# Messages turned by a matmul with the scaled W_o1 in place of a transpose, and an end stretch that joins gelu on POOL

## The chip, the cores and the metric

The kernel runs on one core of a Trainium2 chip. It is measured by the device time of one execution, in microseconds; the median of the runs counts. A core has a matrix engine (PE, with its weight loads shown apart as PEld), a vector engine (DVE), a scalar engine (ACT), a general engine (POOL) and an engine that issues transfers (SP). They run side by side, each in the order of its own instructions, and wait for one another by semaphores. PE writes to PSUM; the other data on the chip is in SBUF.

## The reference

One layer of a graph network, with 12500 nodes of 128 features and 400000 edges sorted by destination (`dst`), in float32:

```python
h = maximum(layernorm(x), 0)
Wij = smu(edge_attr @ W_f1.T + b_f1) @ W_f2.T + b_f2      # edge_attr: (400000, 20)
Wij = Wij * edge_weight[:, None]
x_ij = (h @ W_in2f.T)[dst] * Wij
agg = segment_sum(x_ij, src, 12500)
out = x + smu(agg @ W_o1.T + b_o1) @ W_o2.T + b_o2
```

with `smu(x) = ((1 + a) x + (1 - a) x erf(m (1 - a) x)) / 2`, a = 0.01, m = 2.5. In the kernel this is a gelu plus a straight part: with z = ZS x, smu(x) = GC (gelu(z) + LIN x), where ZS, GC and LIN are constants made of a and m. GC is folded into the weights that follow.

The call takes `x` as (idx_j = dst, idx_i = src): rows of h are gathered by the sorted `dst`, and the sum goes over `src`, which is in no order.

## The kernel before

**Tiles.** The 400000 edges are 3125 tiles of 128. Four tiles are a *group* (782 of them), two groups a *super* (391). The nodes are 98 *bins* of 128. Since `src` has no order, the messages are sorted into bins through DRAM: each message row (128 features and its place in the bin) is scattered to a slot of its bin, and later each bin's rows are read back and summed by a matmul with a selection matrix. This goes by *epochs*: nine of them, of 59, 59, 59, 59, 48, 37, 27, 27 and 16 supers (so 118, 118, 118, 118, 96, 74, 54, 54 and 32 groups), each with a buffer of its own. While epoch k's messages are made and scattered, epoch k-1's are read back and summed. What epoch 8 scattered is read back in the *end stretch*, together with the output.

**A group in the main loop.** The loop over g works on several groups at once:

- `hide(g+2)`: PE, first filter product into `pu` (L551); `bend`: ACT, gelu into `ge` (L559); `smooth`: DVE, straight part added into `sm` (L567)
- `weigh(g+1)`: PE, second filter product into `pw` (L604); `gather(g+1)`: PE, rows of h by a one-hot matrix into `ph` (L585); `take`: ACT copies them to `hg` (L593); `mix(g+1)`: DVE, (pw + b2) * hg into `mt`, features on the partitions (L614)
- `turn(g)`: PE turns the four 128x128 blocks of `mt` into `pt`, edges on the partitions (L624)
- `send(g)`: ACT scales each edge's row by its edge weight into `ms`, which has six buffers (L634); POOL scatters the four tiles by four indirect DMAs (L637) to slots in `ix`
- `bins`, `count`, `read`, `number`: DVE and PE find the slots (L485, L499 to L502, L529, L538)
- `parts(k-1, ...)`: the sums of the epoch before. `fetch` loads `rw` (SP, L668), `choose` makes the selection matrices `se` (DVE, L679), `add` multiplies them (PE, L692) and adds four bins into `agg` (DVE, L705). They start four groups into an epoch (`WAIT`); `choose` for the first chunk stands two groups into it, and waits for the load, which waits for the last scatter of the epoch before.
- `step`: in epoch 0 alone, pieces of the preparation (layernorm, h, loads). `late_loads` is one of them.

Each engine has the order of these calls as written. `pt`, `pu`, `pw`, `ph` and `pc` have one PSUM bank each, `ge`, `sm`, `hg` and `mt` two buffers each.

**The end stretch.** A *unit* is four bins (24 of them) or one of the two last bins. In the loop over the bins of epoch 8, PE sums (L692), and for finished units, one behind the other:

- `first_half`: PE multiplies `agg` by `w_o1` into `pu` or `ph` (L250), ACT takes gelu into `ge` (L251)
- `between`: DVE adds LIN times the product to gelu, into `sm` (L255)
- `second_half`: PE multiplies by `w_o2` into `pw` or `pt` (L260)
- `store`: DVE adds the old rows of x (L264), SP writes out (L266, L268), and then `ask` loads the old rows for the unit four places on: issued by ACT's queue (L240) into `hg` or `mt`, output bias added by POOL (L246)

`between` and `store` are called after the second bin of a unit, `second_half` and `first_half` after the fourth, so a unit passes through three units' time.

**Opening.** Loads are issued from SP, ACT and POOL. `w_o1` is loaded in `late_loads`, from SP. DVE scales `w_f2` by GC there (L764). A path at the end of the program, taken only where a bound of the sorting is exceeded (not with this data), uses `half`, `bent`, `rest` and `stored` too.

Of the kernel before, what the change touches and what calls it, by code (L numbers as in the profile page):

```python
# [9 lines left out]
F32 = mybir.dt.float32  # L10
# [3 lines left out]
AF = mybir.ActivationFunctionType  # L14
ALU = mybir.AluOpType
# [4 lines left out]
P = 128  # L20
# [4 lines left out]
ZS = MU * (1.0 - ALPHA) * math.sqrt(2.0)  # L25
GC = (1.0 - ALPHA) / ZS
LIN = ALPHA / GC

SUP = 8
GRP = 4  # L30
# [9 lines left out]
def gnn_kernel(  # L40
# [19 lines left out]
    nc = tc.nc  # L60
# [9 lines left out]
    def bin_rows(t, b, n):  # L70
        return t[b * P:(b + n) * P, :].rearrange("(b p) f -> p b f", p=P)
# [34 lines left out]
    ident = const.tile([P, P], F32, name="ident")  # L106
# [42 lines left out]
    agg = const.tile([P, NB * P], F32, name="agg")  # L149
# [7 lines left out]
    bz = const.tile([P, 1], F32, name="bz")  # L157
    w_o1 = const.tile([P, P], F32, name="w_o1")
# [29 lines left out]
    def stats(pool, b):  # L188
        st = pool.tile([P, 6], F32, name="st")
        nc.vector.bn_stats(st, x_sb[:, b, :])  # L190
        nc.vector.bn_aggr(mv[:, b, :], st)
# [41 lines left out]
    def width(unit):  # L233
        b, n, rows = unit
        return (n - 1) * P + rows
# [12 lines left out]
    def half(unit, po, ge):  # L248
        w = width(unit)
        nc.tensor.matmul(po[:, :w], w_o1, agg[:, unit[0] * P:unit[0] * P + w], start=True, stop=True)  # L250
        nc.scalar.activation(ge[:, :w], po[:, :w], AF.Gelu, scale=ZS, bias=bz)  # L251

    def bent(unit, po, ge, sm):
        w = width(unit)
        nc.vector.scalar_tensor_tensor(sm[:, :w], po[:, :w], LIN, ge[:, :w], op0=ALU.mult, op1=ALU.add)  # L255

    def rest(unit, sm, py):
        b, n, rows = unit
        for j in range(n):
            nc.tensor.matmul(py[:rows, j, :], sm[:, j * P:j * P + rows], w_o2, start=True, stop=True)  # L260
# [10 lines left out]
    with tc.tile_pool(name="ld", bufs=4) as ld, \  # L271
# [110 lines left out]
        nc.gpsimd.dma_start(w_f1[0:R, :], w_f1_t)  # L382
        nc.gpsimd.dma_start(w_f1[R:R + 1, :], b_f1)
        nc.sync.dma_start(fbufs[0][0:R, :], f_t[:, 0:SUP * P])
        nc.scalar.dma_start(x_sb[:, 1:HEAD, :], bin_rows(x, 1, HEAD - 1))
        nc.gpsimd.dma_start(w_f2, w_f2_t)
        nc.gpsimd.dma_start(b2, b_f2.rearrange("o p -> p o"))
# [14 lines left out]
        def late_loads():  # L402

            nc.sync.dma_start(w_sb[:, CH:NT], w_col[:, CH:NT])
            nc.sync.dma_start(w_o1, w_o1_t)

        def later_loads():
            nc.sync.dma_start(w_o2, w_o2_t)
# [135 lines left out]
        def hide(g):  # L544

            if g >= NG:
                return
            n = groups[g][1] * P
            o = g % PER * GRP * P
            pu = ps1.tile([P, GRP * P], F32, name="pu")  # L550
            nc.tensor.matmul(pu[:, :n], w_f1, loaded[g // PER][0][:, o:o + n], start=True, stop=True)  # L551
            units_of[g] = pu
# [65 lines left out]
        def turn(g):  # L618

            n = groups[g][1]  # L620
            pt = ps1.tile([P, GRP, P], F32, name="pt")
            mt = mixed.pop(g)
            for j in range(n):
                nc.tensor.transpose(pt[:, j, :], mt[:, j * P:(j + 1) * P], ident)  # L624
            mixed[g] = pt

        def send(g):
# [134 lines left out]
        loaded[0] = (fbufs[0], None, h_first.rearrange("p b k d -> p (b k d)"))  # L762
        hide(0)
        nc.vector.tensor_scalar(w_f2, w_f2, GC, None, op0=ALU.mult)  # L764
        for b in range(1, HEAD):
            stats(edge, b)
        deviations(1, HEAD)
# [17 lines left out]
        for s in (1, 2):  # L785
            targets(s)
        turn(0)
        send(0)
        hide(1)
# [51 lines left out]
        for c in range(1, NC):  # L841
# [4 lines left out]
            for f in mine:  # L846
                steps.append(f)
                if c > 1:
                    steps.append(single.pop(0))
        steps += loads + [late_loads, later_loads, last_loads]  # L850
        for i in range(0, len(single), 2):
            steps.append(lambda two=single[i:i + 2]: [f() for f in two])
# [22 lines left out]
        for g in range(NG):  # L875
# [3 lines left out]
            i = g - g0  # L879
# [29 lines left out]
            if g:  # L909
                turn(g)  # L910
                send(g)
# [25 lines left out]
        row_of, ready, opened, smoothed, summed = [], [], [], [], []  # L937
# [11 lines left out]
        turns = [0, 0]  # L949

        def other(i, names):
            turns[i] += 1
            return names[turns[i] % 2]

        def first_half():
            unit = ready.pop(0)
            po = ps1.tile([P, GRP * P], F32, name=other(0, ("pu", "ph")))
            ge = edge.tile([P, GRP * P], F32, name="ge")
            half(unit, po, ge)
            opened.append((unit, po, ge))  # L960

        def between():
            unit, po, ge = opened.pop(0)
            sm = edge.tile([P, GRP * P], F32, name="sm")
            bent(unit, po, ge, sm)
            smoothed.append((unit, sm))

        def second_half():
            unit, sm = smoothed.pop(0)
            py = ps1.tile([P, GRP, P], F32, name=other(1, ("pw", "pt")))  # L970
            rest(unit, sm, py)
            summed.append((unit, py))

# [9 lines left out]
        for c in order_of[k]:  # L983
            for b in range(c * SPAN[k], min(NB, (c + 1) * SPAN[k])):
                for q in range(Q[k]):
                    add(k, b, q)
                if b % GRP == 1:
                    if opened:
                        between()
                    if summed:  # L990
                        store()
                if b % GRP == GRP - 1 or b == NB - 1:
                    ready += [u for u in units if u[0] // GRP == b // GRP]
                    if smoothed:
                        second_half()
                    if len(ready) > 1:
                        first_half()
        while ready or opened or smoothed or summed:
            if smoothed:
                second_half()  # L1000
            if ready:
                first_half()
            if opened:
                between()
            if summed:
                store()
# [16 lines left out]
    with tc.If(flag > 0):  # L1023
        with tc.tile_pool(name="gl", bufs=1) as gl, tc.tile_pool(name="gps", bufs=1, space=PSUM) as gps:
# [11 lines left out]
            with tc.For_i(0, NT, 1) as t:  # L1036
# [26 lines left out]
                                               op1=ALU.mult, accum_out=dup)  # L1063
                pu = gps.tile([P, P], F32, name="gpu")
                nc.tensor.matmul(pu, w_f1[:R + 1, :], fb, start=True, stop=True)
                ge = gl.tile([P, P], F32, name="gge")
                nc.scalar.activation(ge, pu, AF.Gelu, scale=ZS)
                sm = gl.tile([P, P], F32, name="gsm")
                nc.vector.scalar_tensor_tensor(sm, pu, LIN, ge, op0=ALU.mult, op1=ALU.add)
                pw = gps.tile([P, P], F32, name="gpw")  # L1070
# [17 lines left out]
            for b, n in chunks(NB, GRP):  # L1088
                pt = gps.tile([P, GRP * P], F32, name="gpt")
                w = min(N, (b + n) * P) - b * P  # L1090
# [6 lines left out]
        with tc.tile_pool(name="gfin", bufs=1) as fin, tc.tile_pool(name="gfps", bufs=1, space=PSUM) as fps:  # L1097
            for unit in units:
                xr, ys = fin.tile([P, GRP, P], F32, name="xr"), fin.tile([P, GRP, P], F32, name="ys")
                ge, sm = fin.tile([P, GRP * P], F32, name="fge"), fin.tile([P, GRP * P], F32, name="fsm")  # L1100
                po, py = fps.tile([P, GRP * P], F32, name="gpo"), fps.tile([P, GRP, P], F32, name="gpy")
                old_rows(unit, xr, nc.sync)
                with_bias(unit, xr, nc.vector)
                half(unit, po, ge)
                bent(unit, po, ge, sm)
                rest(unit, sm, py)
                stored(unit, py, xr, ys, nc.sync)
# [48 lines left out]
```

## Time and profile before

| | us |
|---|---|
| timed runs, median (three: 4150.53 to 4153.11) | 4151.15 |
| the profiled execution's own time | 4134.27 |
| its span, first to last instruction | 4132.4 |
| busy in it: PE / DVE / POOL / ACT | 3500.0 / 3498.8 / 3048.9 / 1854.6 |
| mean granted TensorE clock | 0.959 |

How to read it. A group line of the profile has the line of the kernel, engine and operation, the tiles it writes and reads, its shape, how many, then the busy time in us, the mean of one in ns, and the idle time of the engine just before them with what ended it. A stretch line has the stretch, its length, the busy time of each engine in it with the number of instructions, the granted clock, the DMA share and GB/s. A timeline line has the start, the duration, the engine and line, and in brackets the idle time before it. Matmuls are pipelined, so the step from one start to the next tells more than the duration of one. An f32 matmul appears as two records, a transpose as one.

POOL by epochs (all its work in the stretch between the starts of the epochs, as it scatters):

| stretch, us | what | PE busy | DVE busy | POOL busy |
|---|---|---|---|---|
| 655 to 1253 | epoch 1 | 505.60 | 497.46 | 454.07 |
| 2448 to 2935 | epoch 4 | 427.22 | 421.00 | 369.64 |
| 2935 to 3309 | epoch 5 | 336.16 | 330.94 | 283.75 |
| 3309 to 3584 | epoch 6 | 252.34 | 249.98 | 207.62 |
| 3584 to 3857 | epoch 7 | 235.34 | 239.84 | 207.11 |
| 3857 to 4024 | epoch 8 | 150.87 | 147.47 | 119.74 |
| 4024 to 4132.4 | end stretch | 92.79 | 74.43 | 32.07 |

### The profile page before, as it was taken

The page shows a single profiled execution, that of the slowest core. Times are in us where ns is not written, and L with a number is a line of the kernel's source. Part 1 is how long each engine was busy: PE and PEld are TensorE (multiplying, and loading weights), DVE is VectorE, ACT ScalarE, POOL GpSimd, SP SyncE. Part 2 cuts the span into 40 slices and gives each one's busy share as a digit, 9 for nine tenths or more (in the row PEclk, how much of TensorE's full clock was granted, in tenths as well). Part 3 has the DMA queues.
Part 4 walks back from the last instruction along what each step waited for, and adds up shares of the span by engine and source line. Part 5 has one row for each costly group of instructions (what it writes and reads, how often), then busy time and mean ns, then how long its engine had stood idle before and what let it go on. Part 6 is the DMA issues. An engine that isn't in the chain of part 4 may idle for free. (4 is left out here: it accounts for less than half of the span.)

```text
span 4132.4 us, 67973 instructions
## 1 busy us (share of the span) xinstructions
PE 3500.0 (85%) x18032; PEld 2218.3 (54%) x18032; DVE 3498.8 (85%) x8551; ACT 1854.6 (45%) x4810; POOL 3048.9 (74%) x3173
## 2 busy tenths in 40 slices
PE   6767886988887888869888879998799889898888
PEld 2334444555554555545555546665466556565567
DVE  6898886988887988869888869998799889898887
ACT  3446553544444444435444434444344444444431
POOL 4777777777777777777777777777777777777772
PEclk8999998999998999989999989999899999999999
DMA  4875665766656766647666647776588689787568
GB/s 144 234 198 174 189 186 176 211 193 193 196 156 200 211 197 190 199 140 214 214 189 194 201 149 209 215 212 199 173 233 230 176 244 248 211 234 219 170 184 240
DMA packets 564967, 820.60 MB, mean 199 GB/s; under 512 B 178779, under 2 KB 379234, under 8 KB 564444
## 3 DMA queue, kind: packets, MB, share of 16 engines
q1 hardware_dynamic: 450650, 602.06, 51.1%
q0 software_dynamic: 100320, 207.40, 15.2%
q10 hardware_dynamic: 13602, 6.73, 0.6%
q8 instruction: 143, 2.34, 0.3%
q14 instruction: 252, 2.06, 0.2%
HBM read 442.51 MB, written 373.37 MB: 197 GB/s over the span
## 5 line engine op out<-in xcount | busy, mean ns | idle before, releaser
L637 POOL DMA_INDIRECT buf<-ms,ix x3125 | 3008.6, 963 | 1006.6 <-issue 424.8
L634 ACT ACTIVATE ms<-pt,w_sb 128x128 f32<-128x128 f32 x3125 | 890.9, 368 | 1442.2 <-PE pt L624 848.6
L692 PEld LDWEIGHTS pg<-se,rw 128*128 128x128 f32 x8036 | 1060.6, 193 | 267.0 <-issue 225.1
L692 PE MATMUL pg<-se,rw 128*128 128x128 f32 x8036 | 1154.2, 281 | 8.5 <-DVE se L679 8.5
L485 DVE SCALAR_TENSOR_TENSOR so<-irow_ps,hi_f,so 128x98 f16<-128x98 f32 x3116 | 989.8, 318 | 82.6
L624 PE MATMUL pt<-ident,mt 128*128 128x128 f32 x3125 | 507.2, 286 | 524.7 <-DVE mt L614 522.0
L604 PE MATMUL pw<-sm,w_f 128*128 128x512 f32 x1564 | 902.9, 660 | 42.6 <-DVE sm L567 40.7
L551 PE MATMUL pu<-f,w_f 128*128 128x512 f32 x1564 | 824.5, 610 | 0.0
L559 ACT ACTIVATE ge<-pu 128x512 f32<-128x512 f32 x782 | 469.1, 600 | 555.4 <-PE pu L551 540.2
L679 DVE TENSOR_TENSOR se<-irow_ps,rw 128x1536 f32<-128x1536 f32 (+1 forms) x345 | 587.8, 1704 | 148.4 <-DMA rw<-buf 147.2
L614 DVE SCALAR_TENSOR_TENSOR mt<-pw,b,hg 128x512 f32<-128x512 f32 x782 | 583.3, 746 | 145.8 <-ACT hg L593 133.9
L624 PEld LDWEIGHTS pt<-ident,mt 128*128 128x128 f32 x3125 | 348.2, 143 | 624.5 <-DVE mt L614 618.2
L567 DVE SCALAR_TENSOR_TENSOR sm<-pu,ge 128x512 f32<-128x512 f32 x782 | 534.9, 684 | 151.6 <-ACT ge L559 147.1
L593 ACT ACTIVATE hg<-ph 128x512 f32<-128x512 f32 x782 | 469.1, 600 | 170.0 <-PE ph L585 99.6
L529 DVE TENSOR_REDUCE sl<-pc 128x4 f32<-128x392 f32 x782 | 434.7, 556 | 0.0
L604 PEld LDWEIGHTS pw<-sm,w_f 128*128 128x128 f32 x1564 | 240.3, 194 | 164.2 <-DVE sm L567 136.4
L585 PE MATMUL ph<-oh,hw 126*128 126x512 bf16 x776 | 306.4, 395 | 0.0
L551 PEld LDWEIGHTS pu<-f,w_f 128*128 128x128 f32 x1564 | 258.7, 199 | 59.5 <-issue 52.0
L499 PE MATMUL pc<-so,tri 128*128 128x392 f16 x782 | 260.6, 333 | 1.9 <-DVE so L485 1.1
L501 PE MATMUL pc<-so,rest_h 128*128 128x294 f16 x781 | 227.4, 291 | 0.0
L501 PEld LDWEIGHTS <-rest_h 128*128 128x128 f16 x781 | 77.1, 99 | 272.4 <-issue 272.3
L460 DVE TENSOR_SCALAR oh<-rbc,prow 128x1024 bf16<-128x1024 bf16 x388 | 192.8, 497 | 1.5 <-DMA rbc<-rel_dram 1.5
(151 smaller groups left out, 1357.5 us busy)
## 6 DMA issues: line engine op xcount, KB each, us to landing
rw<-buf SPq DMA_DIRECT2D x292, 774.0 KB
rbc<-rel_dram SPq DMA_DIRECT2D x389, 256.0 KB
buf<-zero SPq DMA_DIRECT2D x243, 387.0 KB
buf<-ms,ix POOLq DMA_INDIRECT x3125
buf<-zero SPq DMA_DIRECT2D x193, 258.0 KB
rw<-buf SPq DMA_DIRECT2D x49, 645.0 KB
f<-in_f_t SPq DMA_DIRECT2D x390, 80.0 KB
hw<-h_dram SPq DMA_DIRECT2D x776, 31.5 KB
```

The lines of the kernel that those rows point to most:

```text
L485: nc.vector.scalar_tensor_tensor(so[:, j], irow_ps[:, :NB], hi_f[:, t + j:t + j + 1], so[:, j - 1] if j else before, op0=ALU.is_equal, op1 ...
L551: nc.tensor.matmul(pu[:, :n], w_f1, loaded[g // PER][0][:, o:o + n], start=True, stop=True)
L559: nc.scalar.activation(ge[:, :n], units_of[g][:, :n], AF.Gelu, scale=ZS)
L567: nc.vector.scalar_tensor_tensor(sm[:, :n], units_of.pop(g)[:, :n], LIN, hidden[g][:, :n], op0=ALU.mult, op1=ALU.add)
L593: nc.scalar.activation(hg[:, :n], rows_of[g][:, :n], AF.Copy)
L604: nc.tensor.matmul(pw[:, :n], w_f2, hidden.pop(g)[:, :n], start=True, stop=True)
L614: nc.vector.scalar_tensor_tensor(mt[:, :n], pws.pop(g)[:, :n], b2, rows_of.pop(g)[:, :n], op0=ALU.add, op1=ALU.mult)
L624: nc.tensor.transpose(pt[:, j, :], mt[:, j * P:(j + 1) * P], ident)
L634: nc.scalar.activation(ms[:, j, 0:P], pt[:, j], AF.Copy, scale=w_sb[:, t + j:t + j + 1])
L637: i = nc.gpsimd.indirect_dma_start(out=bufs[k][:, :], out_offset=bass.IndirectOffsetOnAxis(ap=ix[:, j:j + 1], axis=0), in_=ms[:, j, :], in ...
L679: nc.vector.tensor_tensor(se[:, :m], irow_ps.unsqueeze(1).to_broadcast([P, m, P]), rows_in[c][:, :m, P:P + 1].to_broadcast([P, m, P]), op= ...
L692: nc.tensor.matmul(pgs[0][:, g, :], rows_in[c][:, o, 0:P], sel[c][:, o, :], start=(q == 0), stop=(q == Q[k] - 1))
```

## The change

W_o1 is applied to each message instead of to each node's sum: `turn` multiplies each block of `mt` by `w_o1` (scaled by LIN once at the opening) instead of turning it by the identity. What is scattered and summed is then LIN times the first output product, so `agg` holds what `pu` or `ph` held in the end stretch, times LIN. In the end stretch `first_half` has no product: ACT takes gelu from `agg` with the scale divided by LIN, and `between` adds `agg` to it on POOL instead of DVE. `second_half` goes around four PSUM banks instead of two. `w_o1` is loaded at the opening from ACT's queue, before the x rows of bins 1 to 3, and no longer from SP in `late_loads`. `half` and `bent`, now used only by the path not taken, have their scales changed to match.

```diff
@@ half, bent
-        nc.scalar.activation(ge[:, :w], po[:, :w], AF.Gelu, scale=ZS, bias=bz)
+        nc.scalar.activation(ge[:, :w], po[:, :w], AF.Gelu, scale=ZS / LIN, bias=bz)
...
-        nc.vector.scalar_tensor_tensor(sm[:, :w], po[:, :w], LIN, ge[:, :w], op0=ALU.mult, op1=ALU.add)
+        nc.vector.tensor_add(sm[:, :w], po[:, :w], ge[:, :w])
@@ opening
         nc.sync.dma_start(fbufs[0][0:R, :], f_t[:, 0:SUP * P])
+        nc.scalar.dma_start(w_o1, w_o1_t)
         nc.scalar.dma_start(x_sb[:, 1:HEAD, :], bin_rows(x, 1, HEAD - 1))
@@ late_loads
             nc.sync.dma_start(w_sb[:, CH:NT], w_col[:, CH:NT])
-            nc.sync.dma_start(w_o1, w_o1_t)
@@ turn
             for j in range(n):
-                nc.tensor.transpose(pt[:, j, :], mt[:, j * P:(j + 1) * P], ident)
+                nc.tensor.matmul(pt[:, j, :], mt[:, j * P:(j + 1) * P], w_o1, start=True, stop=True)
@@ opening
         nc.vector.tensor_scalar(w_f2, w_f2, GC, None, op0=ALU.mult)
+        nc.vector.tensor_scalar(w_o1, w_o1, LIN, None, op0=ALU.mult)
@@ end stretch
         def other(i, names):
             turns[i] += 1
-            return names[turns[i] % 2]
+            return names[turns[i] % len(names)]
+
+        def part_of(unit):
+            return agg[:, unit[0] * P:unit[0] * P + width(unit)]
 
         def first_half():
             unit = ready.pop(0)
-            po = ps1.tile([P, GRP * P], F32, name=other(0, ("pu", "ph")))
             ge = edge.tile([P, GRP * P], F32, name="ge")
-            half(unit, po, ge)
-            opened.append((unit, po, ge))
+            nc.scalar.activation(ge[:, :width(unit)], part_of(unit), AF.Gelu, scale=ZS / LIN, bias=bz)
+            opened.append((unit, ge))
 
         def between():
-            unit, po, ge = opened.pop(0)
+            unit, ge = opened.pop(0)
             sm = edge.tile([P, GRP * P], F32, name="sm")
-            bent(unit, po, ge, sm)
+            nc.gpsimd.tensor_add(sm[:, :width(unit)], part_of(unit), ge[:, :width(unit)])
             smoothed.append((unit, sm))
 
         def second_half():
             unit, sm = smoothed.pop(0)
-            py = ps1.tile([P, GRP, P], F32, name=other(1, ("pw", "pt")))
+            py = ps1.tile([P, GRP, P], F32, name=other(0, ("pu", "ph", "pw", "pt")))
             rest(unit, sm, py)
```

## The prediction

> **What bounds the kernel now.** I read the engines and groups of the page first, then one line at a time by stretches of the span, then the timelines of PE and of the end.
>
> ```profile
> PE 3500.0 (85%) x18032; PEld 2218.3 (54%) x18032; DVE 3498.8 (85%) x8551; ACT 1854.6 (45%) x4810; POOL 3048.9 (74%) x3173
> ...
> L637 POOL DMA_INDIRECT buf<-ms,ix x3125 | 3008.6, 963 | 1006.6 <-issue 424.8
> ...
> L692 PE MATMUL pg<-se,rw 128*128 128x128 f32 x8036 | 1154.2, 281 | 8.5 <-DVE se L679 8.5
> ...
> L624 PE MATMUL pt<-ident,mt 128*128 128x128 f32 x3125 | 507.2, 286 | 524.7 <-DVE mt L614 522.0
> ```
>
> POOL is at 74%, but its scatter does not stop. The same line by stretches:
>
> ```profile
> 670.00:770.00 100.00, 75.91 (x80) 1.00 0.69 202
> ...
> 2945.00:3065.00 120.00, 91.03 (x96) 0.99 0.81 231
> 3320.00:3440.00 120.00, 89.74 (x94) 0.98 0.90 247
> ...
> 3868.00:4012.00 144.00, 102.54 (x107) 0.99 0.68 202
> ```
>
> 120 us hold 96 scatters (91.0 us busy): about 1.26 us each (0.96 and a gap of 0.30, as POOL's timeline shows), 5.055 us for a group of four. 782 groups make 3953 of the 4132 us. So POOL sets the pace of the whole edge part, and PE, DVE and ACT run ahead of it until the six ms buffers are full (ACT's L634 waits 474 us for the scatter to release them). At 3320 and 3868 POOL falls short of its pace: there the producers are late.
>
> How late can they be? At each epoch's start PE loses its lead, as DVE's choose waits for rw until POOL has scattered the last group of the epoch before. From the starts of the L634 groups and of their scatters, the lead is some 20 to 24 us before the starts of epochs 2 to 6 (13, 8 and 14 before 1, 7 and 8), and 5 us after each (ACT L634 resumes at 2944.37 after a wait of 21.31 us, the scatter of that group is at 2950.05). From there the producers must beat 5.055 us a group. Their own pace after each restart, over 18 to 28 groups: epochs 1 to 3, 4.63; epoch 4, 4.81; 5, 4.78; 6, 5.07; 7, 4.79; 8, 5.39. In epoch 0 it is 5.00 (groups 20 to 110), against 5.14 for POOL there. The margin is 0.43 us in epochs 1 to 3, about 0.26 in 4, 5 and 7, none in 6 and 8.
>
> PE's timeline in such a run shows what a group is made of:
>
> ```profile
> 2957.26 1.12 PE L692 MATMUL pg<-se,rw 128*128 128x128 f32 x8
> 2958.22 0.60 PE L624 MATMUL pt<-ident,mt 128*128 128x128 f32 x4
> 2958.66 1.02 PE L604 MATMUL pw<-sm,w_f 128*128 128x512 f32 x2
> 2959.52 0.38 PE L585 MATMUL ph<-oh,hw 126*128 126x512 bf16 x1
> ```
>
> PE has no gap here. A transpose is one record (four of them x4), an f32 matmul two (L604 x2 for one product). Four transposes hold PE from 2958.22 to 2958.66: 0.44 us (0.50 in the group at 3029.61).
>
> **The change, part by part.** (1) *Four transposes become four f32 matmuls with the 128 columns of w_o1.* The nearest row has the same form, stationary slices of sm and 128 columns of w_o2 (L260), in the end stretch:
>
> ```profile
> 4100.94 1.13 PE L260 MATMUL pt<-w_o,sm 128*128 128x128 f32 x8
> ...
> 4101.91 1.02 PE L250 MATMUL pu<-agg,w_o 128*128 128x512 f32 x2
> ...
> 4102.77 1.95 PE L692 MATMUL pg<-se,rw 128*128 128x128 f32 x16
> ...
> 4104.59 1.13 PE L260 MATMUL pw<-w_o,sm 128*128 128x128 f32 x8
> ```
>
> Eight records, 4100.94 to 4101.91: 0.97 us. So +0.47 to +0.53, I take +0.50 us of PE in each of 782 groups. The first send of a group also comes 0.5 us later, which ACT (45% busy) covers.
>
> How much of the 0.50 reaches the pace? PE idles before L624, waiting for DVE's mt, by (idle of the group / number of groups in the window) 0.48 us a group in epoch 0 (58.6/122), 0.40 in 1 to 3, 0.38 in 4, 0.20 in 5, 0.24 in 6, 0.41 in 7, 0.09 in 8. It is concentrated in the groups in which DVE has a choose of 1.7 us (10 waits in 25 groups of epoch 5), and a later PE can swallow it there; in the other groups PE has none. At most all of that idle is swallowed, at least none. I take half, since after a swallowed group DVE's own slack is gone too. So the pace grows by 0.26, 0.30, 0.31, 0.40, 0.38, 0.30 and 0.45:
> - epoch 0: 5.26 against 5.14, 108 groups: +13
> - epochs 1 to 3: 4.93, under 5.055: 0. The lead no longer fills to 23 us, which costs nothing by itself
> - epoch 4: 5.12, 0.07 x 92: +6; epoch 5: 5.18, 0.13 x 70: +9
> - epoch 6: 5.45, 0.40 x 50: +20; epoch 7: 5.09, 0.04 x 50: +2
> - epoch 8, already on PE: 0.45 x 28: +13
> - the 5 us of lead can shrink to the 3.1 us seen in epoch 8 before POOL starves: -2 in each of 4, 5, 6: -6
>
> Main loop: +57. All idle swallowed: epochs 5, 6 and 8 alone, 2 + 14 + 11 - 4 = +23. None: 39 + 26 + 23 + 16 + 26 + 12 + 14 = +156.
>
> L624's rows have one record per block and L260's two, at about 0.11 to 0.12 us each, so the matmul costs twice the transpose here. [...]
>
> (2) *Scaling by LIN.* One DVE instruction of 0.22 us at the opening (row of w_f, L764), and the w_o1 load on ACT's queue, 0.45 us of issue ahead of the x rows. The x rows are used at 10.8 us, where DVE is behind anyway (its L721 waited until 9.0): 0 to +0.5 us, I take 0.3. One SP issue fewer in late_loads: nothing waits for it. Gelu's and the add's other scale cost nothing.
>
> (3) *The end stretch.* Removed are 24 wide products and two narrow ones: L250 holds PE 0.86 us of a unit's 3.65 us (4100.94 to 4104.59), with PE busy 100% from 4035 to 4115. If PE stayed the bound: -0.86 x 24 = -21. But DMA was busy 0.87, 0.97 and 0.84 in the three thirds of that stretch, which leaves some 10% of 80 us: -9 at best. And the add moves to POOL, a new wait. POOL's order is then add(k), bias(k+3), add(k+1), bias(k+4). A bias (L246) waits for its x rows, whose buffer (hg, mt, two each) is released by the store four units before. So add(k+1) stands behind a load that could be issued only after store(k-1), and store(k+1) needs add(k+1): one turn for two units. Queued behind POOL's wait are the add, PE's w_o2 product, and the L692 of the next unit behind that. The rows:
>
> ```profile
> 4093.41 0.68 DVE L264 TENSOR_TENSOR ms<-pw,hg 128x512 f32<-128x512 f32 x1
> 4094.13 0.47 ACTq L240 DMA_DIRECT2D hg<-in_x  x1
> ...
> 4099.76 1.28 POOL L246 TENSOR_TENSOR hg<-hg,bo 128x512 f32<-128x512 f32 x1 [3.28 <-DMA hg<-in_x]
> ```
>
> Store to issue 0.72; issue to bias 5.63 here, 3.36 for the last load (4116.01 to 4119.37); bias 1.21; add 1.27 (L246's form, both operands in SBUF); to PE 0.05; L260 1.16; to the store 0.10. With 3.4 it is 7.9 us, with 5.6 10.1 us for two units: 3.95 to 5.05 a unit against 3.65, +7 to +34. A slower stretch loads the DMA less, so I take 4.15 a unit: +12.
>
> Sum: 57 + 0.3 + 12 = **+69 us** on the execution of 4134.3 (span 4132.4). The timed runs lie higher, median 4151.15; on them I forecast **4220**, 1.7% slower.
>
> **Rivals.**
> *A, the forecast.* Own range +35 to +120. For it: the margins above. 0.68.
> *B, nothing swallowed.* DVE and PE hand each other the delay in every group and the end's loads stay at 5 us: +156 + 27 = +183, 4334. Against it: 10 waits of 25 groups are real slack. 0.10.
> *C, most of it swallowed, and the end a little shorter.* +23 - 9 = +14, about 4165 (from +9 up to +35). For it: DVE is as busy as PE (3499 us each). 0.11.
> *D, faster.* The end decides: PE's 0.86 us a unit is really gained (the loads arrive earlier as w_o1's product no longer delays the stores), -21, while POOL hides the main loop. That needs a surcharge of at most 0.25 us a group, so that epochs 4, 5 and 7 keep to 5.055, and none in 6 and 8, where PE and DVE would have to be swallowing it: with 0.1 a group there, 0.1 x 78 = +8, in all -13, 4138. It decides from under +21 in the main loop. Against it: L260, the full PE of epoch 8, and a DMA share up to 0.97 in the end. 0.06.
> *E, within the bound.* C's main loop and D's end meet at +23 - 21: +2, 4153. 0.04.
> [...] 0.01.
>
> **How the numbers follow.** This kernel can tell 0.2% (8 us) from no change. Faster is D, 0.06; same is E, 0.04; slower is A, B, C and F, 0.90. The range leaves out D and E below and most of B and F above, and takes in most of C: 4162 to 4300.
>
> **What would show it.** L624 with 6250 records and 8 of them in about 0.97 us; POOL's scatters under 95 in 120 us at 2945, 3320 and 3595 and its waits for ACT's ms grown; L624's idle shrunk; epochs 1 to 3 as long as before (598 us each). In the end, L250 gone, L246 or the new add waiting for mt and hg, PE no longer at 100%, a unit at some 4.1 us. I am wrong if POOL keeps 5.055 us through epochs 5 and 6, if epochs 1 to 3 grow, or if a unit of the end takes under 3.65.

## The result, and the profile after

The changed kernel takes 4159.4 us (median of 20 runs, 4152.57 to 4164.91) against 4151.8 of the kernel before (20 runs, 4147.40 to 4158.52) beside it: a ratio of 1.0017, 95% interval 1.0010 to 1.0024. That is +7.6 us: slower, clear of the noise, but by less than the 0.2% (8 us) under which the prediction counts a result as no change. The forecast was +69.

The page of the kernel after, lines as shown before (busy shares; then line, engine, operation, tiles and shape, count, busy us, mean ns, idle us before it and what ended most of it):

```profile
span 4157.5 us, 74090 instructions
...
PE 3687.4 (89%) x21105; PEld 2559.9 (62%) x21105; DVE 3502.6 (84%) x8526; ACT 1832.9 (44%) x4810; POOL 3079.8 (74%) x3199
...
L637 POOL DMA_INDIRECT buf<-ms,ix x3125 | 3009.3, 963 | 1037.0 <-issue 482.0
...
L624 PE MATMUL pt<-w_o,mt 128*128 128x128 f32 x6250 | 887.8, 286 | 374.8 <-DVE mt L614 372.8
...
L692 PE MATMUL pg<-se,rw 128*128 128x128 f32 x8036 | 1149.6, 280 | 9.6 <-DVE se L679 8.3
...
L604 PE MATMUL pw<-sm,w_f 128*128 128x512 f32 x1564 | 826.6, 611 | 8.1 <-DVE sm L567 5.9
```

L624 has twice the records, and PE works 187 us more, yet POOL's idle before its scatters has grown by 30 us only (1006.6 to 1037.0), and epoch 0 alone was 16 us longer in these two executions. The scatters by stretches of the kernel after (stretch, length, POOL busy with the number of scatters, clock, DMA share, GB/s), at the like places of epochs 1, 5, 6 and 8:

```profile
690.00:790.00 100.00, 75.82 (x79) 1.00 0.68 195
2964.00:3084.00 120.00, 91.30 (x95) 0.99 0.82 222
3340.00:3460.00 120.00, 87.91 (x92) 0.99 0.95 239
3895.00:4039.00 144.00, 98.54 (x104) 0.99 0.67 200
```

Epoch 5 still has 95 scatters in 120 us (96 before): POOL keeps its pace there. Only epochs 6 (94 to 92) and 8 (107 to 104) lose some. PE's timeline in epoch 5 of the kernel after (start, duration, both us) shows the new step:

```profile
2971.99 1.12 PE L692 MATMUL pg<-se,rw 128*128 128x128 f32 x8
2972.96 1.16 PE L624 MATMUL pt<-w_o,mt 128*128 128x128 f32 x8
2973.96 1.02 PE L604 MATMUL pw<-sm,w_f 128*128 128x512 f32 x2
2974.82 0.38 PE L585 MATMUL ph<-oh,hw 126*128 126x512 bf16 x1
```

The eight records hold PE from 2972.96 to 2973.96, 1.00 us, as L260 had said (0.97).

Where the time went, by the starts of each epoch's first scatter (us; the end stretch runs from the last scatter's end to the last instruction; the last two rows are experiments told below):

| kernel | epoch 0 | 1 to 3 | 4 | 5 | 6 | 7 | 8 | end |
|---|---|---|---|---|---|---|---|---|
| before | 636.4 | 1792.7 | 486.6 | 374.1 | 275.7 | 272.9 | 167.2 | 107.7 |
| after | 652.8 | 1794.8 | 486.4 | 375.3 | 280.5 | 274.5 | 171.7 | 101.5 |
| difference | +16.4 | +2.1 | -0.2 | +1.2 | +4.8 | +1.6 | +4.5 | -6.2 |
| forecast | +13 | 0 | +4 | +7 | +18 | +2 | +13 | +12 |
| main loop alone changed (f1) | 642.1 | 1794.9 | 486.7 | 374.6 | 280.8 | 274.4 | 172.1 | 108.2 |
| end alone changed (f2) | 637.3 | 1793.6 | 486.5 | 374.1 | 275.4 | 273.7 | 167.8 | 97.9 |

(Of the forecast, the 2 us of lead that can be used up are taken off in epochs 4, 5 and 6.) Epochs 1 to 8 cost +14.0, the end gives back 6.2: +7.8, which is what the medians show. The 16.4 of epoch 0 is not in the medians: the profiled execution of before, 4134.27, was 17 us under its median and under every one of its timed runs (4147.40 at least), that of after, 4159.43, on it. So the profile of before may stem from another chip than its timed runs; f1 and f2, on one chip, show much the same in epochs 1 to 8 (+12.4 in all).

### The profile page after: what moved, and what is told of

It is laid out like the page before. It is cut to its first block, busy times and chain, and to the rows that moved or that the text cites. A ratio compares the mean times of both kernels' runs of the same rounds, so it can differ in the third digit from the quotient of the medians.

```text
span 4157.5 us, 74090 instructions
## 1 busy us (share of the span) xinstructions
PE 3687.4 (89%) x21105; PEld 2559.9 (62%) x21105; DVE 3502.6 (84%) x8526; ACT 1832.9 (44%) x4810; POOL 3079.8 (74%) x3199
## 4 chain that ended last, share of the span: by engine, by line
PE 39%; DVE 29%; DMA 18%; issue 5%; ACT 5%; POOL 3%; SPq 1%; DVEq 0%; POOLq 0%; ACTq 0%
DMA buf<-ms,ix 15%; PE pt L624 11%; PE pg L692 9%; PE pw L604 8%; DVE se L679 8%; PE pu L551 7%; DVE mt L614 5%; DVE so L485 5%; DVE sm L567 3%; DVE sl L529 3%; ACT ge L559 2%; POOL buf L637 2%; PE ph L585 2%; ACT ms L634 2%; DVE agg L705 1%
## 5 line engine op out<-in xcount | busy, mean ns | idle before, releaser
L637 POOL DMA_INDIRECT buf<-ms,ix x3125 | 3009.3, 963 | 1037.0 <-issue 482.0
L634 ACT ACTIVATE ms<-pt,w_sb 128x128 f32<-128x128 f32 x3125 | 890.8, 368 | 1580.1 <-PE pt L624 1072.5
L624 PE MATMUL pt<-w_o,mt 128*128 128x128 f32 x6250 | 887.8, 286 | 374.8 <-DVE mt L614 372.8
L692 PEld LDWEIGHTS pg<-se,rw 128*128 128x128 f32 x8036 | 1053.1, 192 | 253.8 <-issue 217.3
L692 PE MATMUL pg<-se,rw 128*128 128x128 f32 x8036 | 1149.6, 280 | 9.6 <-DVE se L679 8.3
L624 PEld LDWEIGHTS pt<-w_o,mt 128*128 128x128 f32 x6250 | 773.1, 195 | 461.7 <-DVE mt L614 453.5
L604 PE MATMUL pw<-sm,w_f 128*128 128x512 f32 x1564 | 826.6, 611 | 8.1 <-DVE sm L567 5.9
L551 PE MATMUL pu<-f,w_f 128*128 128x512 f32 x1564 | 811.7, 601 | 0.0
L551 PEld LDWEIGHTS pu<-f,w_f 128*128 128x128 f32 x1564 | 252.8, 195 | 57.1 <-issue 51.2
L604 PEld LDWEIGHTS pw<-sm,w_f 128*128 128x128 f32 x1564 | 242.6, 196 | 20.2 <-DVE sm L567 19.6
```

Of the source, the lines that this page charges most:

```text
L604: nc.tensor.matmul(pw[:, :n], w_f2, hidden.pop(g)[:, :n], start=True, stop=True)
L624: nc.tensor.matmul(pt[:, j, :], mt[:, j * P:(j + 1) * P], w_o1, start=True, stop=True)
L634: nc.scalar.activation(ms[:, j, 0:P], pt[:, j], AF.Copy, scale=w_sb[:, t + j:t + j + 1])
L637: i = nc.gpsimd.indirect_dma_start(out=bufs[k][:, :], out_offset=bass.IndirectOffsetOnAxis(ap=ix[:, j:j + 1], axis=0), in_=ms[:, j, :], in ...
L692: nc.tensor.matmul(pgs[0][:, g, :], rows_in[c][:, o, 0:P], sel[c][:, o, :], start=(q == 0), stop=(q == Q[k] - 1))
```

## The experiments

Two theories stood after the result. One: the main loop costs what PE's surplus leaves over POOL's pace, and the surplus that reaches the pace is far smaller than forecast. The other: the main loop is about as dear as forecast and the end gains more. And for the end: its unit is set by the turn of load, bias, add and store on POOL (as forecast), or by the loads themselves.

| run | changed against before | before there, us | this, us | ratio (95%) |
|---|---|---|---|---|
| e1_before_again | nothing | 5256.5 | 5263.8 | one run |
| e2_main_only | f32 matmul by the identity | 5256.5 | 5252.6 | 0.9979 (0.9953 to 1.0004) |
| e3_end_only | all but `turn` | 5256.5 | 5264.3 | 1.0000 (0.9974 to 1.0027) |
| e4_add_on_dve | the change, add on DVE | 5256.5 | 5257.0 | 0.9989 (0.9958 to 1.0019) |
| f1_main_only | as e2 | 4138.4 | 4153.0 | 1.0035 (1.0021 to 1.0048) |
| f2_end_only | as e3 | 4138.4 | 4130.2 | 0.9981 (0.9972 to 0.9990) |
| g1_add_on_dve | as e4 | 5257.2 | 5229.8 | 0.9935 (0.9905 to 0.9965) |
| g2_six_x_buffers | the change, six x buffers | 5257.2 | 5234.5 | 0.9959 (0.9929 to 0.9989) |
| g3_three_x_buffers | the change, three x buffers | 5257.2 | 5234.6 | 0.9959 (0.9922 to 0.9995) |
| g4_transposes_twice | each transpose made twice | 5257.2 | 5226.9 | 0.9935 (0.9904 to 0.9966) |
| h1_no_x_rows | the change, no rows of x | 5228.8 | 5182.0 | one run |
| h2_transposes_twice | as g4 | 5228.8 | 5193.2 | 0.9942 (0.9914 to 0.9969) |
| h3_add_on_dve | as e4 | 5228.8 | 5183.5 | 0.9920 (0.9892 to 0.9948) |
| k1_transposes_twice | as g4 | 4154.0 | 4159.5 | 1.0014 (1.0004 to 1.0023) |
| k2_add_on_dve | as e4 | 4154.0 | 4151.2 | 0.9997 (0.9988 to 1.0006) |

Each letter is one chip, and a ratio is good only within its own. On three of the five (e, g, h) every kernel, the unchanged one too, takes 5168 to 5310 us; the last section is about that. There the main loop has another bound, and more work on PE shortens it (0.9935 in g4, 0.9942 in h2), so whole times from there (0.992 to 1.000 for the change in its forms) say nothing of the parts; these are read on chips f and k. The end stretch is nearly as long on all of them (unchanged: 107.7 on the first chip, 109.7 on e) and can be read on each.

**One part alone.** `e2` and `f1` change one line of before, and keep its end stretch:

```diff
-                nc.tensor.transpose(pt[:, j, :], mt[:, j * P:(j + 1) * P], ident)
+                nc.tensor.matmul(pt[:, j, :], mt[:, j * P:(j + 1) * P], ident, start=True, stop=True)
```

`e3` and `f2` are the change with that line put back to the transpose, so W_o1 is applied nowhere.

> The kernel before, unchanged, with a second profile. Theory: the first profile of before (span 4132.4) was a low draw of epoch 0, whose waits for transfers vary from run to run; this one has its epoch 1 start (scatter of group 118) some 10 to 20 us later than 655.6, a span of 4140 to 4155, and epochs 1 to 8 and the end as long as in the first profile (3369 us from there to the last scatter, then 107.7 us) within 3 us. Rival: epoch 0 is as short as before (655.6 +- 4), so that the changed kernel's 17 us more in epoch 0 belong to the change.

> The main loop's part alone: the four transposes become four f32 matmuls with the identity, the end stretch as before. Theory (PE's part is paid only where POOL is not ahead): epochs 1 to 8 grow by 14 us as in the changed kernel's profile, epoch 0 by 0 to 5, the end by 0: +12 to +20 us, about 4167. Rival 1 (POOL hides the main loop): within +-4 us of before. Rival 2 (as predicted): +50 or more.

> The end's part alone: transposes by the identity as before, and the changed end stretch. W_o1 is left out of the computation (agg goes to gelu as it is). Theory: main loop as before, the end 101.5 us in place of 107.7 from the last scatter: -5 to -8 us. Rival 1 (the add on POOL behind the loads makes the end slower, as predicted): +7 or more. Rival 2 (the product's time is really gained): -15 to -21.

> The same kernel as e2 (the four transposes of a group become four f32 matmuls with the identity, the end stretch as before), in the hope of a chip on which before takes its 4150 us again; on the chip of e1 to e4 it took 5256 and the producers waited elsewhere. Theory (PE's part is paid only where POOL is not ahead): epochs 1 to 8 grow by 14 us as in the changed kernel's profile, epoch 0 by 0 to 5, the end by 0: +12 to +20 us on 4152. Rival 1 (POOL hides the main loop): within +-4 us of before. Rival 2 (as predicted): +50 or more. If before takes over 5000 us here too, both theories say no difference beyond 0.3%.

> The same kernel as e3 (transposes as before, and the changed end stretch; W_o1 is left out of the computation), on a chip as in f1. Theory: main loop as before, the end 101.5 us in place of 107.7 from the last scatter: -5 to -8 us. Rival 1 (the add on POOL behind the loads makes the end slower, as predicted): +7 or more. Rival 2 (the product's time is really gained): -15 to -21.

On chip e the three could not be told apart; e1's expectation, 4140 to 4155 us, and e2's +12 to +20 were missed there. On chip f the main loop alone costs +14.6 us and the end alone gives -8.2: +6.4 together, the +7.6 of the change within the intervals. By the table of epochs, f1 against f2 on one chip differ by +4.8 in epoch 0, +1.3 in 1 to 3, +0.2, +0.5, +5.4, +0.7 and +4.3 in 4 to 8, and +10.3 in the end. So neither part is as forecast: the main loop costs a quarter of its +57, and the end has the other sign.

**What in the main loop costs.** `g4`, `h2` and `k1` keep the transposes and make each twice:

```diff
-            for j in range(n):
+            for j in [*range(n), *range(n)]:
                 nc.tensor.transpose(pt[:, j, :], mt[:, j * P:(j + 1) * P], ident)
```

> The kernel before with each block of a group transposed twice into the same place, four more transposes of 0.11 us: PE +0.43 us a group, against +0.29 measured for the change (L624 +0.39, L604 -0.10). Theory: some 0.55 of PE's extra reaches the pace, as in f1, and POOL hides what is left under 5.055 us: epochs 1 to 5 +0 to +2 each, 6 +11, 7 +2, 8 +7, epoch 0 +5 to +10, in all +20 to +32 us. Rival 1 (all of it reaches the pace): epochs 4, 5 and 7 grow too by 10 us or more, +60 or more. Rival 2 (the cost of f1 lies in the second weight loads of the f32 matmul, not in PE time as such): +0 to +8 us.

> The same kernel as g4 (each block of a group transposed twice, PE +0.43 us a group), on a chip on which before takes 4150 us. Theory: some 0.55 of PE's extra reaches the pace, as in f1, and POOL hides what is left under 5.055 us: epochs 1 to 5 +0 to +2 each, 6 +11, 7 +2, 8 +7, epoch 0 +5 to +10, in all +20 to +32 us. Rival 1 (all of it reaches the pace): epochs 4, 5 and 7 grow too by 10 us or more, +60 or more. Rival 2 (the cost of f1 lies in the second weight loads of the f32 matmul, not in PE time as such): +0 to +8 us. On a chip on which before takes 5250 us, as under g4, it is faster than before by up to 1%.

> The same kernel as g4 and h2 (each block of a group transposed twice, PE +0.43 us a group), once more for a chip on which before takes 4150 us. Theory: some 0.55 of PE's extra reaches the pace, as in f1, and POOL hides what is left under 5.055 us: epochs 1 to 5 +0 to +2 each, 6 +11, 7 +2, 8 +7, epoch 0 +5 to +10, in all +20 to +32 us. Rival 1 (all of it reaches the pace): epochs 4, 5 and 7 grow too by 10 us or more, +60 or more. Rival 2 (the cost of f1 lies in the second weight loads of the f32 matmul, not in PE time as such): +0 to +8 us. On a chip on which before takes 5200 us: faster than before by about 0.6%, as in g4 and h2.

The page of k1 and then PE's timeline in it, epoch 5:

```profile
L624 PE MATMUL pt<-ident,mt 128*128 128x128 f32 x6250 | 853.4, 281 | 392.9 <-DVE mt L614 390.3
```

```profile
2976.26 1.12 PE L692 MATMUL pg<-se,rw 128*128 128x128 f32 x8
2977.22 1.04 PE L624 MATMUL pt<-ident,mt 128*128 128x128 f32 x8
2978.09 1.02 PE L604 MATMUL pw<-sm,w_f 128*128 128x512 f32 x2
```

Eight transposes hold PE for 0.87 us here, 0.90 on average over 24 groups after a restart, where the four matmuls hold it for 0.945. So nearly all of it is the number of records, not what they compute. Epochs 6 and 8 are 279.0 and 171.7 us (f1: 280.8 and 172.1), and the own pace is that of f1 to within 0.07. The time as a whole grew by 5.6 us, though, where f1's grew by 14.6 on its chip: the theory's +20 to +32 was missed, and the number lies in the range of its rival 2, the second weight loads. The run can't decide against that rival, as making each transpose twice doubles the weight loads too (L624's, 6250 against 3125). No execution of before was profiled on chip k, so where the other 9 us went there is open.

**What sets the end.** The add moved to DVE, in `e4`, `g1`, `h3` and `k2`:

```diff
-            nc.gpsimd.tensor_add(sm[:, :width(unit)], part_of(unit), ge[:, :width(unit)])
+            nc.vector.tensor_add(sm[:, :width(unit)], part_of(unit), ge[:, :width(unit)])
```

More or fewer buffers for the old rows of x, in `g2` (the third name is the one-hot tile, free by then, its three buffers read as f32) and `g3`:

```diff
-                name = ("hg", "mt")[len(wanted) % 2]
+                name = ("hg", "mt", "oh")[len(wanted) % 3]
...
-        for _ in range(4):
+        for _ in range(6):
```

```diff
-        for _ in range(4):
+        for _ in range(3):
```

And no loads of x at all in `h1` (POOL keeps an add of the same form, x is missing from the output):

```diff
-                old_rows(unit, xr, nc.scalar)
-                with_bias(unit, xr, nc.gpsimd)
+                b, n, rows = unit
+                twice = bo2[:rows].unsqueeze(1).to_broadcast([rows, n, P])
+                nc.gpsimd.tensor_add(xr[:rows, :n], twice, twice)
```

> The changed kernel with the add of the end stretch back on DVE. Theory: POOL's turn (load, bias, add, product, store) sets the end's pace of 3.5 us a unit; with the add on DVE a unit takes 2.8 to 3.2 us, the end shrinks by another 6 to 14 us, and the time is 4145 to 4154. Rival: DMA sets that pace (share 0.98 in the changed end); the end stays at 101 us, the time at 4159 +- 3.

> The changed kernel with the add of the end stretch on DVE in place of POOL. Theory: the add's place behind POOL's bias, which waits for x rows, sets the changed end's pace of 3.5 us a unit; on DVE a unit takes about 3 us, the end from the last scatter shrinks from 101.5 to 90 to 97 us, and the kernel stands at -4 to +3 us against before (main loop +14.6, end -12 to -18). Rival: DMA sets that pace (share up to 0.98): end 99 to 102, +6 to +9 us against before.

> The changed kernel with the add on POOL, but six old-row buffers asked for in advance in place of four (the third pair in the idle oh tiles). A load then has five units of time in place of three. Theory: bias and add no longer wait for loads, POOL needs 2.5 us a unit, and the end is as in g1, 90 to 97 us: -4 to +3 us against before. Rival (DMA sets the pace): 99 to 102, +6 to +9 us.

> The changed kernel with three old-row buffers asked for in advance in place of four. The turn of load, bias, add, product and store then spans two units, as the prediction had it for the change itself. Theory: 9 to 10 us for two units, 4.3 to 5 us a unit, the end 118 to 130 us: +24 to +36 us against before. Rival (the turn does not bind): the end stays at 98 to 102, +6 to +9 us.

> The changed kernel, in whose end stretch the old rows of x are not loaded (x is left out of the output; POOL writes twice the output bias in their place, an instruction of the same form and size). It takes 256 KB of some 1.04 MB a unit from the DMA and the wait for loads from POOL's turn. Theory now (DMA sets the changed end's pace: share 0.91, and six, four or three row buffers make no steady difference in e3, g2, g3): a unit falls to PE's 2.7 us, the end from the last scatter to 82 to 88 us. Rival (DVE's and POOL's hand-over by semaphores sets 3.4 us a unit): the end stays at 96 to 102 us.

> The same kernel as e4 and g1 (the changed kernel with the add on DVE; there the end took 97 us against 104 with the add on POOL and 109.7 in before). On a chip on which before takes 4150 us. Theory: the end 91 to 96 us in place of 107.7, the main loop +14.6: -4 to +3 us against before. Rival: the end as in the changed kernel, +6 to +9 us.

> The same kernel as e4, g1 and h3 (the changed kernel with the add on DVE; its end took 97 us there), once more for a chip on which before takes 4150 us. Theory: the end 91 to 97 us in place of 107.7, the main loop +14.6: -4 to +3 us against before. Rival: the end as in the changed kernel, +6 to +9 us. On a chip on which before takes 5200 us: faster than before by 0.6 to 0.8%, as in g1 and h3.

| end stretch | us (chip) |
|---|---|
| unchanged | 107.7, 108.2 (f), 108.7 (k), 109.7 (e), 109.0 (h) |
| the change, four buffers | 101.5, 97.9 (f), 104.2 (e) |
| six buffers; three buffers | 104.3 (g); 99.9 (g) |
| add on DVE | 95.6 (k), 97.3 (e), 97.0 (g), 96.5 (h) |
| no rows of x | 84.3 (h) |

If the turn over POOL set the unit, six buffers should shorten the end and three lengthen it, as g2's and g3's theories said. Neither did: 104.3 and 99.9 lie about the 97.9 to 104.2 of four. But the traces show that neither run changed the turn as it was meant to. With four buffers, a load starts after the store four units before, and its bias stands in POOL's order ahead of the add of the third unit after that store. With six, the bias moved forward with the load: for `hg` and `mt` it still stands ahead of the add of the third unit after the store that let its load start (for `oh`, of the fourth). With three, a load still starts after the store four units before, since `hg` and `mt` have two buffers each, and its bias stands ahead of the add of the third or fourth unit after it. So these two runs don't decide whether the turn sets the unit.

Without the loads, POOL still has two adds a unit, and every unit takes 2.68 us (L692 at 5130.00, 5132.68, ...), PE without a gap. So POOL's own work is no bound, and what the end has over 84.3 us comes with the loads, by their traffic or by the waits for them. The engines in the middle of the end stretch (stretch, length, then busy us and count of PE, PEld, DVE, ACT and POOL, clock, DMA share, GB/s), of before, after, k2 and h1 in this order:

```profile
4040.00:4115.00 75.00, 75.00 (x535) 64.31 (x535) 60.70 (x76) 14.43 (x21) 25.50 (x20) 1.00 0.92 269
```

```profile
4072.00:4146.00 74.00, 60.78 (x516) 58.30 (x515) 51.74 (x59) 16.02 (x23) 52.74 (x44) 1.00 0.92 280
```

```profile
4069.00:4137.00 68.00, 61.39 (x516) 58.50 (x515) 62.31 (x80) 15.80 (x22) 26.08 (x21) 1.00 1.00 299
```

```profile
5112.00:5168.00 56.00, 56.00 (x504) 56.00 (x503) 49.19 (x58) 15.58 (x22) 47.52 (x42) 1.00 0.91 263
```

PE was the bound before (75.00 of 75) and is so in h1 (56.00 of 56). In between, with the loads and without W_o1's product, PE has gaps. In the kernel after, PE waits for POOL's add, and POOL, busy 52.74 of 74 us, waits most of the rest for rows of x (what waits, for what: us in all, times, longest):

```profile
POOL hg L246 <- DMA hg<-in_x: 9.8, 6, 2.5
POOL mt L246 <- DMA mt<-in_x: 8.4, 7, 2.6
```

With the add on DVE no add stands behind those waits, and the end takes 95.6 to 97.3 us on four chips, against 97.9 to 104.2 with the add on POOL (97.3 against 104.2 on chip e, which has both). There the DMA engines are busy the whole time (1.00, 299 GB/s; 0.92 with the add on POOL). But so is DVE: 62.31 of 68 us, and nearly all the rest it waits for ACT's gelu, none of it for a transfer:

```profile
DVE sm L968 <- ACT ge L962: 5.7, 8, 0.7
```

So with the add on DVE it is DVE that sets the unit, as far as its trace shows; that the DMA would be a floor just below isn't shown. With the add on POOL, whether the turn through POOL's order or the pace of the loads sets it is open. `k2` takes the change's whole cost away (0.9997), but it doesn't beat the kernel before either.

## Why the prediction was wrong, step by step

**Right: POOL sets the pace.** Epochs 1 to 3 stayed (+2.1 in 1793), epochs 6 and 8 paid, and in epochs 4, 5 and 7 the pace after the restart kept under 5.055 (4.95 to 4.99). Rival F, with its 0.01, took a cost for an f32 block that no run shows: four blocks took 0.945 us against 0.55, 1.7 times.

**Wrong, the step that failed: "+0.50 us of PE in each of 782 groups", of which half the idle before L624 is swallowed, "so the pace grows by 0.26" to 0.45.** It grew by 0.12 to 0.20, as PE's net surcharge (L624's more and L604's less, told below) was +0.28 to +0.34 and not +0.50. Own pace over the 24 groups after a restart (epoch 6: groups 645 to 690; 8: its 28; 0: groups 20 to 110), in us:

| epoch | 0 | 1 | 4 | 5 | 6 | 7 | 8 |
|---|---|---|---|---|---|---|---|
| before | 5.00 | 4.63 | 4.81 | 4.78 | 5.07 | 4.79 | 5.39 |
| after | 5.16 | 4.83 | 4.95 | 4.96 | 5.19 | 4.99 | 5.57 |
| growth | 0.16 | 0.20 | 0.14 | 0.18 | 0.12 | 0.20 | 0.18 |
| forecast | 0.26 | 0.30 | 0.31 | 0.40 | 0.38 | 0.30 | 0.45 |

(Epoch 0 is the least sure: from f2 to f1, on one chip, it went from 5.07 to 5.09 only. The prediction also read the lead before epoch 1 as 13 us; the trace has 24. Its sum doesn't use it.)

PE's time per group from start to start, without its idle, in the same groups of epochs 1 to 7, and the idle gave three parts:
- L624 took 0.54 to 0.55 before, not 0.44 to 0.50: I had read two groups with low values, while six groups in ten take 0.60. It takes 0.945 after: +0.39.
- L604 took 0.94 to 0.98 before and takes 0.86 to 0.88 after: -0.07 to -0.10. This is a wait that I had not counted. L604's weights are DVE's `sm`, and their load stood waiting for it while L624 still ran, which no idle of PE shows. The waits of before, and of after (engine, tile and line, what is waited for: us in all, times, longest):

```profile
PEld pw L604 <- DVE sm L567: 136.4, 492, 1.3
...
PE pw L604 <- DVE sm L567: 40.7, 82, 1.1
```

```profile
PEld pw L604 <- DVE sm L567: 19.6, 57, 1.3
...
PE pw L604 <- DVE sm L567: 5.9, 19, 1.1
```

A longer L624 hides it: 117 us of the weight loads' wait and 35 of PE's are gone. The mean record of L604 fell from 660 to 611 ns. In before, the load waited in 577 of the last 651 groups, for `sm` in most, and there the first of L604's two records took 0.533 us to the second (median), in the others 0.432, as it does in nearly all groups of after.
- The idle before L624 fell by 0.07 to 0.16 a group (epoch 1: 0.39 to 0.30; epoch 5: 0.18 to 0.06), less than the half of it that I took in epoch 1 (0.20), about that half in epoch 5 (0.10).

In epoch 1, +0.39 - 0.10 - 0.09 = +0.20, in epoch 6, +0.40 - 0.07 - 0.16 = +0.17 (and 0.04 less in L551 and L692), as measured: 0.20 and 0.12.

With these measured paces the prediction's own scheme gives the result (a check after the fact). Epochs 4, 5 and 7 stay under 5.055: 0 (measured -0.2, +1.2, +1.6). Epoch 6, 0.13 x 50 less 2 of lead: +4.5 (+4.8). Epoch 8, 0.18 x 28: +5.0 (+4.5). Epoch 0, 5.16 against POOL's 5.14, x 108: +2 (+4.8 from f2 to f1). The margins decided: in epochs 4, 5 and 7 they were some 0.26, which hides a growth of 0.14 to 0.20 whole and one of 0.30 to 0.40 not.

**Wrong: "I take 4.15 a unit: +12" in the end.** The end got 6.2 us shorter (8.2 by f2's median). I had read POOL's order as add, bias, add, bias and the chain through it as one turn for two units. The end of the kernel after, in its timeline (start, duration, in brackets the idle before it and what ended it):

```profile
4112.55 0.69 DVE L264 TENSOR_TENSOR ms<-pw,hg 128x512 f32<-128x512 f32 x1
...
4113.27 0.47 ACTq L240 DMA_DIRECT2D hg<-in_x  x1
...
4116.50 1.28 POOL L968 TENSOR_TENSOR sm<-agg,ge 128x512 f32<-128x512 f32 x1
...
4119.87 1.27 POOL L246 TENSOR_TENSOR hg<-hg,bo 128x512 f32<-128x512 f32 x1 [2.10 <-DMA hg<-in_x]
...
4121.10 1.27 POOL L968 TENSOR_TENSOR sm<-agg,ge 128x512 f32<-128x512 f32 x1
4122.42 1.16 PE L260 MATMUL ph<-w_o,sm 128*128 128x128 f32 x8 [1.43 <-POOL sm L968]
```

The pieces are as the prediction put them: store 4112.55, issue 4113.27, bias 4119.87 (6.60 later, longer than the 5.63 I had), add, product, and PE waits 1.43 for it. But POOL's order isn't written by hand (only those of PE, DVE, ACT and SP are, so the order of the calls as written holds for these four alone), and in POOL's one more add stands ahead: this store (tile `pw`) is of the third unit before the one whose product (tile `ph`) it holds up, as stores of `pt` and `pu` lie between. The turn, 9.87 us from store to product, spans three units, not two: L692 starts at 4111.87, 4116.37, 4119.05 and 4123.42, a unit of 2.7 to 4.5, over the middle of the end 3.41 in the mean, under the 3.65 of before. So the forecast "-9 at best", from a DMA share that left 10% of 80 us, was the right size for the end (-6.2 to -10.3), and rival C had it. In part that was luck: with the add on DVE the end got some 12 to 13 us shorter (95.6 against 108.7 on chip k, 97.3 against 109.7 on e), so that share was no bound. Its two halves, most of the surplus swallowed and a somewhat shorter end, are what happened: +14 forecast, with +23 in the main loop where f1 had +14.6. The whole, +7.6, lies just under the +9 at which C's own range began.

**The opening**, +0.3, is too small to be seen beside the scatter of epoch 0.

## What to carry to other kernels

An engine's idle time is only part of its slack. A weight load that waited during the matmul ahead of it showed up as longer matmuls here (L604's mean record, 660 ns before and 611 after): look in the waits for the weight loads too, and take the mean step over many groups, not from one.

When another engine sets the pace, set the margin of each stage against the surcharge that reaches its pace; where the two are alike, the forecast hangs on tenths of a microsecond and its range must reach down to nothing.

A chain through an engine whose order is not written by hand can't be laid out from the program alone, and an experiment that is to lengthen or shorten it may leave it as it was: read from the trace which instruction stands ahead of which before concluding from the time.

## What the runs showed of the hardware

**Two kinds of chips.** On chips e, g and h the kernel before takes 5229 to 5257 us, some 26% more than on the others, in all epochs of the main loop (epoch 1: 762.7 against 597.8). Its scatters do not come at POOL's pace there: 64 in 100 us, against 79 at the same place in the profile of before. A stretch of epoch 1 in e1 (POOL busy and count, clock, DMA share, GB/s), then the clock after an idle, PE's timeline first:

```profile
1020.00:1120.00 100.00, 61.37 (x64) 0.88 0.49 157
```

```profile
2005.18 1.11 PE L624 MATMUL pt<-ident,mt 128*128 128x128 f32 x4 [4.68 <-issue]
2006.09 1.92 PE L604 MATMUL pw<-sm,w_f 128*128 128x512 f32 x2
```

```profile
2004.00:2007.00 3.00, 1.82 (x6) 1.30 (x7) 2.52 (x7) 1.50 (x5) 2.23 (x3) 0.50 0.72 246
```

The records give one sign: L634, which writes an `ms` buffer again, started a median 30 us after the last packet seen of the scatters that had held it (those of six groups earlier), against 5 us in the profile of before. But under a third of the DMA landings are recorded there (23639 against 76442), so this isn't settled, and why these chips differ is open.

**More work on PE made the kernel faster there.** With each transpose made twice it took 0.994 of the time (0.9904 to 0.9966, and 0.9914 to 0.9969 on another chip), and the clock of the profiled executions was 0.902 (g4) and 0.901 (h2), against 0.873 (e1). The rows above show a link: after 4.68 us of idle the clock is 0.50 and L604 takes 1.92 instead of 1.02 us. The trace of the kernel after has it too: the eight records of L624 hold PE for 1.87 us after an idle of 21.68 us (from 681.63, clock 0.50), and for 1.00 us after one of 1.22 us (from 717.24, clock 1.00). After idles of like length between, the trace has both: after 3.23 us they took 1.86 us (from 2243.67, clock 0.50), after 3.27 us 1.00 us (from 1716.28, clock 1.00). No run separates the number of records from the shorter idles that they leave (before L624, PE is idle for 960 us in all in e1 and for 879 in h2, on two chips). That the clock alone made the gain wasn't tried.

**Epoch 0** took 636 to 653 us in the profiles of the faster chips, with 637 to 642 on one chip and 647 to 651 on another. Its differences between kernels of different chips say nothing.
